# Row sums of attention weights over pairs of key chunks, added on GpSimd, in a two-layer graph-attention kernel

## Chip, cores, metric

One NeuronCore of a Trainium2 chip. The metric is the device time of one execution in microseconds (us). All runs quoted of one kernel agree within 0.3%. PE is the matmul engine (TensorE), DVE VectorE, ACT ScalarE, POOL GpSimd.

## The reference, cut to what matters

32 graphs of 512 nodes and 256 features go through two layers. Both have 8-head attention masked by the graph's adjacency; the first also has an MLP. All data is fp32, except the integer adjacency.

```python
# layer 0: allowed = (adj > 0) | (adj^T > 0) | eye ; layer 1: allowed = adj != 0
scores = einsum('bhqd,bhkd->bhqk', q * scale, k)
attn   = softmax(where(allowed, scores, -inf))
ctx    = einsum('bhqk,bhkd->bhqd', attn, v)
x = layernorm(x + ctx @ Wo.T + bo) ; x = layernorm(x + mlp(x))      # layer 0
x = layernorm(x + layer(x))                                        # after each layer
```

## The kernel before

A slot is the attention of one graph in one layer. It has eight chunks: two groups of four heads, each with four chunks of 128 keys. Scores are computed transposed (keys on partitions), so a softmax row sum is a sum over partitions, and PE makes it with a block of ones.

```python
def scores(self, layer, k):
    ...                                        # four matmuls into one PSUM tile of 4 banks
    p = work.tile([P, HPC, N], F32, tag="p", bufs=4)
    nc.scalar.activation(p, s, AF.Exp, scale=SCALE)
def masked(self, layer, k):                    # p *= 0/1 mask, on VectorE
    nc.vector.tensor_tensor(p, p, m[:, k % NQ, None, :].to_broadcast([P, HPC, N]), ALU.mult)
def product(self, layer, k):
    for j in range(HPC): nc.tensor.matmul(a[...], self.v[...], p[:, j, :], ...)   # values (psA)
    for j in range(HPC): nc.tensor.matmul(s[...], ones, p[:, j, :], ...)          # row sums (psR)
    ...                                        # after four chunks: sT, r, rT, cT divide on VectorE
def statistics(self, y, n, i):
    ...
    nc.gpsimd.tensor_scalar(rs, mv[:, 1:2], EPS, None, ALU.add)                   # rs on GpSimd
    nc.gpsimd.tensor_tensor(rs, rs, neg_half[:, 0:1], ALU.pow)
```

Every slot is interleaved with other work, so that PE has something to do while ScalarE and VectorE work on the weights. In an **MLP slot** (F in the prediction) it is the rest of another graph's layer 0: output projection, MLP, three layer norms. In a **mask slot** (O) it is the end of another graph's layer 1, and the masks of a new graph. Four slots form the cycle: mask, MLP, MLP, mask.

norm1, norm2 and norm3 are the three layer norms of layer 0, norm4 is that of layer 1; a number in brackets is one of four blocks of 128 rows. rs is the reciprocal of a row's standard deviation, which each norm waits for. bov is a bias row added to x.

## Time and profile before

| | before |
|---|---|
| median of 3 runs | 3851.9 us (3851.83 to 3852.65) |
| busy PE / DVE / ACT / POOL | 94 / 65 / 42 / 36% |
| MLP slot / mask slot | 70.3 / 49.4 and 48.3 us (two mask slots in a row) |
| granted PE clock | 0.992 |

The granted clock is the share of the full PE clock that the trace shows as granted. In these traces it is either full or half, and half comes in stretches of 3.4 us or two or three times that (at the very end of a run, other lengths). Counted over the whole trace, from the first output projection of one slot to that of the next, all 32 MLP slots of before take 70.3 us without such a stretch. Of 30 mask slots (the first and the last left out) 15 have none and take 48.3 us, and 15 have one and take 49.1 to 49.3. So the 49.4 above is a mask slot with a low clock.

The prediction below shows the lines. A line of the page's groups gives the source line, engine, operation, tiles and shapes, then busy time and mean duration, then the idle time ahead of the group and who ended it. In a timeline the first number is the start, the second the duration in us. In a chain of waits each piece is start, duration, what ran.

### The profile page before, as it was taken

How to read it: one execution, taken by the hardware profiler on the slowest of the kernel's cores; microseconds unless marked ns; L12 is line 12 of the kernel's file. 1: busy time of each engine (PE TensorE's matmuls, PEld its weight loads, DVE VectorE, ACT ScalarE, POOL GpSimd, SP SyncE). 2: the span in 40 equal slices, each digit the busy share in tenths (PEclk: the TensorE clock that was granted, in tenths of full speed). 3: DMA queues.
4: the chain of work that ended last, by engine and by line, in shares of the span. 5: the costliest groups of instructions: out<-in, count | busy, mean ns of one | idle time of the engine just before them, and what ended most of it. 6: DMA issues, size and time to landing. Idle time of an engine off the chain costs nothing.

```text
span 3851.9 us, 51652 instructions
## 1 busy us (share of the span) xinstructions
PE 3608.8 (94%) x21514; PEld 1885.4 (49%) x21514; DVE 2502.6 (65%) x3461; ACT 1603.0 (42%) x1729; POOL 1376.5 (36%) x1545
## 2 busy tenths in 40 slices
PE   6999999999999999999999999998999999999998
PEld 3544536455364554635546355453554535545354
DVE  3666675766757667576665756667576675666766
ACT  3434444434444344343443444434444344343443
POOL 1333333433334243342433424333242333424332
PEclk9999999999999999999999999999999999999999
DMA  2000000000000000000000000000000100000000
GB/s 86 17 23 13 27 12 17 23 23 17 12 17 23 22 23 6 17 28 17 23 6 17 28 17 23 6 22 23 17 23 6 33 12 17 23 6 34 12 1 12
DMA packets 57553, 75.61 MB, mean 20 GB/s; under 512 B 4448, under 2 KB 40416, under 8 KB 57312
## 3 DMA queue, kind: packets, MB, share of 16 engines
q1 hardware_dynamic: 51776, 67.90, 5.2%
q10 hardware_dynamic: 5536, 4.33, 0.4%
q8 instruction: 170, 2.79, 0.3%
q14 instruction: 71, 0.58, 0.0%
HBM read 55.45 MB, written 16.78 MB: 19 GB/s over the span
## 4 chain that ended last, share of the span: by engine, by line
PE 69%; DVE 23%; POOL 5%; ACT 2%; issue 1%; DMA 0%; ACTq 0%; DVEq 0%; POOLq 0%
PE psQK L260 12%; PE psF L391 12%; PE psH L373 12%; DVE p L282 9%; PE psS L273 8%; PE psA L295 7%; PE psV L245 6%; PE psR L303 6%; PE psO L352 5%; POOL rs L330 4%; DVE st L328 3%; DVE x L411 2%; DVE m L214 2%; ACT p L277 2%; DVE y L341 2%; PE psT L233 1%
## 5 line engine op out<-in xcount | busy, mean ns | idle before, releaser
L277 ACT ACTIVATE p<-psS 128x2048 f32<-128x2048 f32 x512 | 961.9, 1879 | 1167.1 <-PE psS L273 1167.1
L282 DVE TENSOR_TENSOR p<-p,m 128x2048 f32<-128x2048 f32 x512 | 1197.4, 2344 | 273.4 <-ACT p L277 273.4
L330 POOL TENSOR_SCALAR rs<-mv 128x1 f32<-128x1 f32 x512 | 499.2, 975 | 1115.0 <-DVE mv L329 1100.3
L295 PE MATMUL psA<-p,v 128*32 128x512 f32 x4096 | 555.8, 615 | 53.6 <-DVE p L282 53.6
L273 PE MATMUL psS<-qT,kT 32*128 32x512 f32 x4096 | 583.9, 640 | 7.1 <-ACT p L277 2.0
L303 PE MATMUL psR<-p,ones 128*32 128x512 f32 x4096 | 544.6, 604 | 0.0
L314 DVE STREAM_TRANSPOSE sT<-psR 128x512 f32<-128x512 f32 x128 | 91.3, 713 | 643.8 <-PE psR L303 643.8
L391 PE MATMUL psF<-w_L_gnn_W,hT 128*128 128x256 f32 x2048 | 459.1, 382 | 0.0
L373 PE MATMUL psH<-xT,w_L_gnn_W 128*128 128x256 f32 x2048 | 459.1, 382 | 0.0
L391 PEld LDWEIGHTS psF<-w_L_gnn_W,hT 128*128 128x128 f32 x2048 | 383.8, 190 | 100.7 <-ACT cT L311 26.8
L373 PEld LDWEIGHTS psH<-xT,w_L_gnn_W 128*128 128x128 f32 x2048 | 383.8, 190 | 98.2 <-ACT xT L236 24.3
L317 POOL TENSOR_TENSOR total<-total,sT 128x16 f32<-128x16 f32 x128 | 29.0, 227 | 985.6 <-DVE sT L314 985.6
L331 POOL TENSOR_TENSOR rs<-rs,neg_half 128x1 f32<-128x1 f32 x512 | 327.1, 639 | 42.7
L273 PEld LDWEIGHTS psS<-qT,kT 32*128 32x128 f32 x4096 | 159.9, 182 | 332.4 <-issue 187.0
L303 PEld LDWEIGHTS psR<-p,ones 128*32 128x32 f32 x4096 | 135.3, 112 | 314.7 <-issue 305.4
L381 ACT ACTIVATE hT<-psH,c_L_gnn_b 128x256 f32<-128x256 f32 x512 | 215.1, 471 | 171.3 <-PE psH L373 169.2
L260 PE MATMUL psQK<-xT,w_L_gnn_Wqkv 128*128 128x512 f32 x512 | 245.0, 611 | 0.0
L252 ACT COPY v<-psV 128x512 f32<-128x512 f32 x128 | 75.0, 586 | 403.3 <-PE psV L245 403.3
L352 PE MATMUL psO<-w_L_gnn_Wo,cT 128*128 128x256 f32 x1024 | 238.4, 386 | 0.5 <-DVE held L768 0.5
L352 PEld LDWEIGHTS psO<-w_L_gnn_Wo,cT 128*128 128x128 f32 x1024 | 189.2, 190 | 72.3 <-ACT kT L263 47.8
L341 DVE TENSOR_TENSOR y<-psO,x 128x256 f32<-128x256 f32 x256 | 104.1, 407 | 152.5 <-PE psO L352 152.5
L295 PEld LDWEIGHTS psA<-p,v 128*32 128x32 f32 x4096 | 80.9, 108 | 230.1 <-issue 101.9
(64 smaller groups left out, 3476.9 us busy)
## 6 DMA issues: line engine op xcount, KB each, us to landing
adj<-in_adj_dram SPq DMA_DIRECT2D x32, 1024.0 KB, 6.2
x<-in_x_dram SPq DMA_DIRECT2D x32, 512.0 KB, 3.9
out_dram<-x SPq DMA_DIRECT2D x32, 512.0 KB, 2.9
w_L_gnn_W<-in_L_gnn_W_dram ACTq DMA_DIRECT2D x2, 1024.0 KB, 10.8
w_L_gnn_Wqkv<-in_L_gnn_Wqkv_dram SPq DMA_DIRECT2D x1, 768.0 KB, 5.0
w_L_gnn_Wo<-in_L_gnn_Wo_dram ACTq DMA_DIRECT2D x2, 256.0 KB, 5.5
s_L_gnn_bo<-in_L_gnn_bo_dram ACTq DMA_DIRECT2D x2, 128.0 KB, 5.7
s_L_gnn_ln_g<-in_L_gnn_ln_g_dram ACTq DMA_DIRECT2D x2, 128.0 KB, 8.4
```

Source lines behind the costliest of these rows:

```text
L245: nc.tensor.matmul(ps[:, j, :], self.xT[:, i, at], proj[layer][0][2][:, i, :], start=(i == 0), stop=(i == ND - 1),)
L260: nc.tensor.matmul(ps, w[:, i, c * P : (c + 1) * P], self.xT[:, i, :], start=(i == 0), stop=(i == ND - 1))
L273: nc.tensor.matmul(s[:, j, :], self.kT[at, hg, kc * P : (kc + 1) * P], self.qT[at, hg, :], start=True, stop=True)
L277: nc.scalar.activation(p, s, AF.Exp, scale=SCALE)
L282: nc.vector.tensor_tensor(p, p, m[:, k % NQ, None, :].to_broadcast([P, HPC, N]), ALU.mult)
L295: nc.tensor.matmul(a[j * HD : (j + 1) * HD, :], self.v[:, kc, h * HD : (h + 1) * HD], p[:, j, :], start=(kc == 0), stop=(kc == NQ - 1),)
L303: nc.tensor.matmul(s[j * HD : (j + 1) * HD, :], ones, p[:, j, :], start=(kc == 0), stop=(kc == NQ - 1))
L330: nc.gpsimd.tensor_scalar(rs, mv[:, 1:2], EPS, None, ALU.add)
L331: nc.gpsimd.tensor_tensor(rs, rs, neg_half[:, 0:1], ALU.pow)
L352: nc.tensor.matmul(ps[:, j, :], self.cT[:, k, at], wo[layer][:, k, :], start=(k == 0), stop=(k == ND - 1))
L373: nc.tensor.matmul(ps[:, j, :], w1[:, c, at], self.xT[:, c, h * 2 * P : (h + 1) * 2 * P], start=(c == 0), stop=(c == ND - 1),)
L391: nc.tensor.matmul(ps, self.hT[h][:, f, j * P : (j + 1) * P], w2[:, f, :], start=(f == 0), stop=(f == NF - 1))
```

## The change

The intent: PE is busy 94% of the time, and row sums are 15% of its busy time (544.6 of 3608.8 us). GpSimd adds the weights of two chunks in place, so that one row sum serves both, for three of four pairs. Six weight buffers keep the weights long enough. To relieve VectorE, ScalarE empties the layer 1 mask from PSUM. The preparation of the mask codes goes to the end of the slot.

```diff
-                code = self.tile("edge", [NQ, N], BF16, bufs=1)
+                edge = self.tile("edge", [NQ, N], BF16, bufs=1)
+                none = self.tile("none", [NQ, N], BF16, bufs=1)
                 for i in range(NQ):
...
+                    nc.gpsimd.tensor_scalar(none[:, i, :], self.adj[:, i, :], 0.0, None, ALU.is_equal)
...
-                nc.vector.tensor_scalar(self.m1[:, i, :], ps, 0.0, None, ALU.not_equal)
+                nc.scalar.activation(self.m1[:, i, :], ps, AF.Copy, bias=1.0, scale=-1.0)
...                                  # p bufs 4 -> 6; xT, sT, rT bufs 2 -> 1; z bufs 3 -> 2
+            def pair(self, k):
+                nc.gpsimd.tensor_tensor(self.p[k], self.p[k], self.p[k + 1], ALU.add)
+            def sums(self, k, first=False, last=False):
...                                  # the ones matmuls and the division, out of product()
             # MLP slot, second half
             last.norm2(2)
             last.norm3(1)
-            g.product(layer, 4)
+            g.sums(2, last=True)     # and with it the division for heads 0 to 3
+            g.product(4)
             g.scores(layer, 7)
             last.norm2(3)
...
-            g.product(layer, 5)
             last.transpose(last.x2, 0)
-            g.product(layer, 6)
+            g.product(5)
+            g.pair(4)
             last.value(1, 0)
+            g.product(6)
             last.transpose(last.x2, 1)
-            g.product(layer, 7)
+            g.sums(6, first=True)
...
+            g.product(7)
+            g.sums(7)
+            g.sums(4, last=True)
             last.value(1, 1)
+            if later is not None:
+                later.code()         # was after residual1 (MLP slot), before the last multiply (mask slot)
...                                  # MLP slot, first half: pair(0) after product 1, pair(2) before hidden(1, ...)
...                                  # mask slot: pair(0), pair(2), pair(4) after products 0, 2, 5
```

## The prediction

> **What bounds the kernel now.** I read the page first (busy times, then the chain that ended last), then the stage table of four consecutive attention slots, the timeline of those slots, and the chain of waits inside them.
>
> ```profile
> PE 3608.8 (94%) x21514; PEld 1885.4 (49%) x21514; DVE 2502.6 (65%) x3461; ACT 1603.0 (42%) x1729; POOL 1376.5 (36%) x1545
> ...
> PE 69%; DVE 23%; POOL 5%; ACT 2%; issue 1%; DMA 0%; ACTq 0%; DVEq 0%; POOLq 0%
> ...
> L282 DVE TENSOR_TENSOR p<-p,m 128x2048 f32<-128x2048 f32 x512 | 1197.4, 2344 | 273.4 <-ACT p L277 273.4
> L330 POOL TENSOR_SCALAR rs<-mv 128x1 f32<-128x1 f32 x512 | 499.2, 975 | 1115.0 <-DVE mv L329 1100.3
> ...
> L303 PE MATMUL psR<-p,ones 128*32 128x512 f32 x4096 | 544.6, 604 | 0.0
> ```
>
> PE looks like the bound (94% busy), but 28% of the chain is DVE and POOL. A one-element POOL instruction (L330) averages 975 ns, so POOL is waiting inside its own instructions. The program has 64 slots (32 graphs, two layers), in a cycle of four: two that carry another graph's MLP (F) and two that carry a new graph's masks (O). The stage table has, per slot: span, then busy PE, PEld, DVE, ACT, POOL, and the granted clock; its last line is 8 us inside an O slot.
>
> ```profile
> 1999.86:2070.24 70.38, 68.63 (x389) 40.51 (x385) 42.74 (x68) 28.97 (x36) 24.46 (x30) 1.00 0.07 23
> 2140.49:2189.89 49.40, 44.88 (x293) 18.58 (x289) 35.77 (x40) 21.07 (x18) 20.70 (x18) 0.97 0.04 11
> 2189.89:2238.20 48.31, 43.23 (x290) 18.13 (x289) 35.39 (x40) 21.07 (x18) 14.78 (x14) 1.00 0.04 12
> ...
> 2166.00:2174.00 8.00, 6.05 (x39) 2.54 (x32) 8.00 (x7) 1.88 (x1) 4.48 (x4) 0.79 0.01 3
> ```
>
> An F slot is PE bound except for some 7 us of DVE chain after the MLP. In an O slot the chain runs on DVE and POOL without a break from 2191.83 to 2221.14, 29.3 of 48.3 us: PE waits there. So PE time saved in O is worth nothing, and DVE time is worth everything. Now the timeline of the same O slot (start, duration):
>
> ```profile
> 2202.19 2.37 POOL L169 TENSOR_TENSOR x<-x,bov 128x1024 f32<-128x1024 f32 x1
> 2204.64 4.48 POOL L169 TENSOR_TENSOR x<-x,s_L_gnn_ln_b 128x1024 f32<-128x1024 f32 x1
> ...
> 2202.26 2.46 DVE L411 TENSOR_SCALAR x<-y,mv,rs 128x256 f32<-128x256 f32 x1 [0.45 <-POOL rs L331]
> 2204.63 2.28 DVE L282 TENSOR_TENSOR p<-p,m 128x2048 f32<-128x2048 f32 x1
> 2206.83 0.68 DVE L214 TENSOR_SCALAR m<-psM 128x512 bf16<-128x512 f32 x1
> ...
> 2208.03 3.24 DVE L282 TENSOR_TENSOR p<-p,m 128x2048 f32<-128x2048 f32 x1
> ```
>
> L411 normally takes 0.41 us; begun just after the POOL add, it ends with it, after 2.46. The second POOL add needs 4.48 instead of 2.37 because the DVE multiply (2.28) began first; the next multiply takes 3.24 instead of 2.28 because it waits for that add. L214, which reads PSUM, is not held up. The two engines take turns, whole instruction by whole instruction.
>
> **What the Trainium skill says.** "SBUF — State Buffer", section "Who interferes with whom": a DVE instruction with two SBUF inputs, or in a two-port mode, and a GpSimd instruction that reads SBUF exclude each other; the later one blocks until the first is done. The lines above agree. "GPSIMD Engine Reference", section 3.1: a 2048-element fp32 add takes 4497 ns on GpSimd. The trace has 2.36 us for 1024 elements and 0.22 us for 16, so about 2.12 ns per element and 4.5 us for 2048, an estimate that agrees. "TensorE: Matmul & The Clock Gate", Part 1: an idle PE loses half its clock, and needs activity to get it back. The 0.79 above, after 2 us of idle PE, agrees in kind: there a product and its row sum took 3.3 us instead of 1.86.
>
> **The change part by part.**
> 1. Row sums: eight chunks per slot become five products. In the chain one is 0.86 us, so 3 x 0.86 = 2.6 us of PE per slot, 165 us in all, if nothing else binds.
> 2. Adds: three per slot, 4.5 us each: 13.5 us per slot, 864 us over the run. Each shuts out the mask multiplies, the affine steps (L336, L337), the two-port normalizations (L404, L411) and cT (L321).
> 3. Layer 1 mask: 4 x 0.60 us leave DVE in an O slot (2.4 us on the chain), 0.59 us each arrive on ScalarE (42% busy): free.
> 4. "none": four POOL passes of 1.03 us more per graph. The whole code, 8.2 us, moves to the end of a slot, so it stands in the POOL queue ahead of the next O slot's first rs.
> 5. The division for the first four heads (sT, r, rT, cT: 2.4 us of DVE) moves in F from the idle stretch at 2030 to behind the second paired sum, so into the busy DVE stretch after the MLP.
> 6. Six p buffers: no wait for a p buffer shows before, so no gain by themselves.
>
> *F slot, walked by hand* on the times of the slot at 1999.86. The first row sum saved brings nothing: the third score product waits for exp (1.89 us at 2004.71) anyway; the second brings 0.45. The first add follows rs of tile 3 at 2013.1 and holds the port to 2017.75, so the last affine ends at 2018.7 and the transpose starts 0.3 later than before. The third saved sum makes mlp(3) end 0.5 us earlier, at 2045.5. Then DVE: first x2 tiles to 2048.6, the moved division to 2051.0, norm2(3) and the multiply for chunk 6 end at 2054.9 (2052.92 before). rs of tile 3 ends at 2055.6 and the third add follows at once, to 2060.1; norm3(3) waits for it exactly as L411 does above, so the second x2 transpose starts at 2060.5. Left on PE: 0.45 transpose, 3 x 0.86 sums, 3.63 query/key, 1.0 product, 1.73 value, with gaps 9.5: end 2070.0 against 2064.47. **+5.5 us.**
>
> *O slot*, from its first score product S (2134.71 in the first one). Before, the last m1 ends at S+37.6. Now the code passes and the multiply for chunk 0 alternate to S+10.7, the multiply for chunk 1 ends at S+13.0, then the add of bov (layer 1 slots only) at S+15.4, so norm4(1) ends at S+17.95 (before S+13.3). Chunk 2 ends at S+22.2. The first add takes S+22.95 to 27.45, with norm4(3) behind it. Then turns: chunk 3 to 29.9, residual add to 32.3, chunk 4 to 34.5, residual add to 36.9, chunk 5 to 39.1, second add to 43.6. Only then the paired sum on PE (44.5), which the DVE division waits for. The third add starts when r is in (S+45.8) and lasts to 50.4; cT, chunk 6 and m0 of tile 3 end at S+54.0, and the value product needs that PSUM buffer. PE tail: 1.73 + 1.0 + 0.86 + 3.63 + 1.0 + 2 x 0.86 + 1.73 = 11.7, end S+65.8 against S+49.4. **+16.4 us**; in the other O slot, without bov, about +14.8.
>
> Sum: 32 x 5.5 = 176; 31 x 15.6 = 484; lower PE clock after 4.5 to 6.5 us of idle PE, some 1.4 us (3.3 - 1.86) in each O and half that often in F: 65. Total 725 us: 4577, rounded to **4560 us**.
>
> **The rivals.** *A, PE stays the bound and the adds hide on a POOL that is 36% busy:* 3852 - 165 and up to 80 more for the shorter DVE chain: 3610 to 3690. For it: 94% PE, and much of POOL's 1376 us is waiting. Against it: the port, not POOL, is what is scarce, and the waiting POOL time is the proof. *B, the adds collide only in part*, because they settle into the DVE-free half of the F slot (2018 to 2034 has few two-input DVE instructions) and only the O slots lose, some 8 us each: near 4100. For it: the second F add does fall there. Against: the third F add starts right behind the rs that norm3(3) also waits for, and there is no free stretch in O. *C, port plus clock:* long PE idles keep the clock low through most O slots: up to 4800.
>
> **Range and chances.** The walk has errors of perhaps 2 us per F slot and 4 per O slot, mostly shared by all slots: 4380 to 4720. Slower by over 2%: 0.93; within 2%: 0.03; faster: 0.04 (rival A, if the exclusion were weaker for these adds than for L169).
>
> **What would show it.** L303 with 2560 matmuls instead of 4096. A new POOL add, 128x2048, with an uncontended time of 4.5 us and a mean above 6. L282's mean up from 2344 to over 3000 ns, L404 and L411 well over 1000. PE busy share down to about 80%, DVE and POOL shares of the chain far up, F slots near 76 us and O slots near 64. The prediction is wrong if L282 keeps 2.3 us beside a running add, if the adds fall where DVE has no two-input work, or if an add takes much less than 4.5 us.

## The result

The changed kernel takes 4573.7 us (median of 4 runs, 4572.74 to 4574.72) against 3851.9 us in the same rounds. The ratio is 1.187 (95% interval 1.185 to 1.189): it is 19% slower.

From the page of the changed kernel: busy times, chain shares, and the groups that answer to those of before (multiply, the new add, row sums):

```profile
PE 3706.6 (81%) x19978; PEld 1901.0 (42%) x19978; DVE 3160.4 (69%) x3333; ACT 1667.7 (36%) x1857; POOL 2592.1 (57%) x1865
...
DVE 41%; PE 41%; POOL 14%; issue 2%; DVEq 0%; POOLq 0%
...
L284 DVE TENSOR_TENSOR p<-p,m 128x2048 f32<-128x2048 f32 x512 | 1492.8, 2921 | 134.0 <-ACT p L279 134.0
...
L306 POOL TENSOR_TENSOR p<-p,p 128x2048 f32<-128x2048 f32 x192 | 1001.1, 5214 | 6.9 <-PE psA L292 4.3
...
L314 PE MATMUL psR<-p,ones 128*32 128x512 f32 x2560 | 381.0, 690 | 22.4 <-POOL p L306 22.4
```

The row sums fell from 4096 matmuls to 2560 as intended, but PE is only busy 81%, and it is busy longer in all. The multiply grew by 577 ns on average. DVE's share of the chain went from 23 to 41%, POOL's from 5 to 14%.

The stage table, slot by slot (span, busy PE, PEld, DVE, ACT, POOL, granted clock, DMA): mask, MLP, MLP, and the mask slot that came before these three.

```profile
2305.08:2367.10 62.02, 44.98 (x269) 19.14 (x268) 45.45 (x37) 23.18 (x22) 39.64 (x25) 0.86 0.03 9
2367.10:2445.51 78.41, 70.34 (x364) 40.19 (x364) 51.89 (x69) 28.89 (x36) 39.42 (x33) 0.93 0.06 21
2445.51:2523.91 78.40, 70.25 (x362) 40.17 (x361) 53.25 (x68) 28.88 (x36) 41.06 (x34) 0.93 0.02 7
...
2240.60:2305.08 64.48, 45.68 (x265) 19.17 (x264) 47.43 (x36) 23.17 (x22) 42.04 (x27) 0.87 0.08 25
```

Both kinds of slot got longer: the MLP slot from 70.3 to 78.4 us, the mask slots from 48.3 and 49.4 to 62.0 and 64.5. The clock fell too: from 1.00 to 0.93 in MLP slots, from 1.00 and 0.97 to 0.86 and 0.87 in mask slots, and from 0.992 to 0.904 over the run. Every slot of the changed kernel has a low stretch.

Where the time sits is seen in the timeline of one mask slot (POOL lines, then DVE lines):

```profile
2261.45 4.51 POOL L306 TENSOR_TENSOR p<-p,p 128x2048 f32<-128x2048 f32 x1
...
2272.63 6.58 POOL L306 TENSOR_TENSOR p<-p,p 128x2048 f32<-128x2048 f32 x1
...
2283.18 4.50 POOL L306 TENSOR_TENSOR p<-p,p 128x2048 f32<-128x2048 f32 x1
...
2261.51 4.60 DVE L418 TENSOR_SCALAR x<-y,mv,rs 128x256 f32<-128x256 f32 x1 [0.45 <-POOL rs L338]
...
2275.34 6.01 DVE L284 TENSOR_TENSOR p<-p,m 128x2048 f32<-128x2048 f32 x1
...
2283.71 4.53 DVE L328 TENSOR_TENSOR cT<-cT,rT 128x512 f32<-128x512 f32 x1
```

Each of the three adds has a DVE instruction that starts after it and ends just when the add (or, for the multiply, the add and the multiply itself) is done. L418 needs 0.41 us by itself, L328 0.69. The second add waited 2.07 us for the multiply before it, which is not shown (6.58 instead of 4.51), and the next multiply waited 3.8 us for that add.

And in the chain of waits of an MLP slot, from the third add on:

```profile
2428.53 4.59 DVE x L411
...
2433.17 0.90 PE psT L235 x3
2434.07 1.87 PE psR L314 x8
2435.94 4.94 PE psQK L262 x8
```

The third add ran from 2428.47 to 2432.97; the last normalization (L411) waited for it, and PE for the normalization. After this pause the row sum takes 1.87 us (0.86 before the change) and the query and key products 4.94 (3.63 before the change). The granted clock from 2428.5 to 2441.0 is 0.60.

### The profile page after: what moved, and what is told of

It is laid out like the page before. It is cut to its first block, busy times and chain, and to the rows that moved or that the text cites. A ratio compares the mean times of both kernels' runs of the same rounds, so it can differ in the third digit from the quotient of the medians.

```text
span 4572.0 us, 48806 instructions
## 1 busy us (share of the span) xinstructions
PE 3706.6 (81%) x19978; PEld 1901.0 (42%) x19978; DVE 3160.4 (69%) x3333; ACT 1667.7 (36%) x1857; POOL 2592.1 (57%) x1865
## 4 chain that ended last, share of the span: by engine, by line
DVE 41%; PE 41%; POOL 14%; issue 2%; DVEq 0%; POOLq 0%
DVE p L284 14%; PE psF L398 10%; PE psQK L262 8%; PE psR L314 5%; PE psH L380 5%; DVE cent L343 4%; POOL rs L337 4%; POOL none L197 4%; PE psV L247 4%; DVE cT L328 4%; DVE x L418 3%; PE psA L292 3%; DVE x L411 3%; PE psS L275 3%; DVE st L335 3%; POOL rs L338 2%
## 5 line engine op out<-in xcount | busy, mean ns | idle before, releaser
L284 DVE TENSOR_TENSOR p<-p,m 128x2048 f32<-128x2048 f32 x512 | 1492.8, 2921 | 134.0 <-ACT p L279 134.0
L306 POOL TENSOR_TENSOR p<-p,p 128x2048 f32<-128x2048 f32 x192 | 1001.1, 5214 | 6.9 <-PE psA L292 4.3
L337 POOL TENSOR_SCALAR rs<-mv 128x1 f32<-128x1 f32 x512 | 471.9, 922 | 833.3 <-DVE mv L336 819.2
L292 PE MATMUL psA<-p,v 128*32 128x512 f32 x4096 | 592.1, 652 | 74.5 <-DVE p L284 74.5
L314 PE MATMUL psR<-p,ones 128*32 128x512 f32 x2560 | 381.0, 690 | 22.4 <-POOL p L306 22.4
L247 PE MATMUL psV<-w_L_gnn_Wqkv,xT 128*128 128x256 f32 x512 | 179.0, 511 | 222.2 <-DVE m L216 222.2
L235 PE MATMUL psT<-ident,x 128*128 128x128 f32 x768 | 167.0, 329 | 212.9 <-DVE x L411 111.9
L348 DVE TENSOR_TENSOR y<-psF,x 128x256 f32<-128x256 f32 x128 | 54.4, 425 | 360.7 <-PE psF L398 360.7
L343 DVE SCALAR_TENSOR_TENSOR cent<-y,mv,s_L_gnn_ln_g 128x256 f32<-128x256 f32 x256 | 256.6, 1002 | 0.0
L235 PEld LDWEIGHTS psT<-ident,x 128*128 128x128 f32 x768 | 96.0, 158 | 378.3 <-DVE y L348 127.2
```

The source lines that it names most:

```text
L292: nc.tensor.matmul(self.acc[hg][j * HD : (j + 1) * HD, :], self.v[:, kc, h * HD : (h + 1) * HD], self.p[k][:, j, :], start=(kc == 0), stop ...
L306: nc.gpsimd.tensor_tensor(self.p[k], self.p[k], self.p[k + 1], ALU.add)
L314: nc.tensor.matmul(self.total[j * HD : (j + 1) * HD, :], ones, self.p[k][:, j, :], start=first, stop=last)
L343: nc.vector.scalar_tensor_tensor(c, y, stats[0], g, ALU.subtract, ALU.mult)
```

## The experiments

The theory: the adds and the DVE instructions that the prediction names (those with two inputs in SBUF, and the normalizations, which it calls two-port) exclude each other, the places of the adds are on DVE's chain, and PE time is hardly worth anything there. The rivals: PE time is what counts; GpSimd is just slow, so whoever waits for its results or stands behind them in its line waits long; or the new order, not the adds, costs.

| run | median us | ratio to before |
|---|---|---|
| before | 3850.9 to 3852.1 | 1 |
| changed | 4573.7 | 1.187 |
| a_no_adds | 3988.2 | 1.036 |
| b_fills | 4267.0 | 1.108 |
| c_no_third | 4296.7 | 1.116 |
| d_code_back | 4523.7 | 1.175 |
| e_adds_dve | 4133.5 | 1.073 |
| f_mask_scalar | 3799.5 | 0.987 |
| g_division_early | 4518.3 | 1.173 |
| h_one_pair | 3773.0 | 0.980 |
| i_dummy_free | 3851.5 | 1.000 |
| j_dummy_tail | 3955.5 | 1.027 |
| k_fewer_sums | 3836.3 | 0.996 |
| l_buffers | 3852.2 | 1.000 |

### What the saving is worth: k_fewer_sums

```diff
-                for j in range(HPC):              # row sums, in the kernel before
+                for j in range(HPC) if k not in (1, 2, 5) else ():
```

> The kernel before with the row sums of chunks 1, 2 and 5 simply left out (five instead of eight per slot, as in the change; wrong result on purpose), nothing added. It prices the saving by itself. Theory (saved PE time counts only where PE sets the end): in an MLP slot 0.45 us for chunk 1 (exp ends soon after), 0.86 for chunk 2, nothing for chunk 5 and nothing in a mask slot: 32 x 1.3 = 42 us less, 3810, 3790 to 3830; more PE idle may cost some of it through the clock. Rival (PE busy 94% is the bound): 165 us less, 3687.

Measured: 3836.3 us, 15.7 us less (ratio 0.9961, 0.9947 to 0.9975). The rival's 165 us are excluded, and even the theory's 42 were too many. Two consecutive MLP slots with the two mask slots between them, from the stage table:

```profile
2057.92:2127.00 69.08, 66.06 (x364) 39.67 (x361) 42.74 (x68) 28.74 (x36) 26.79 (x34) 1.00 0.07 24
...
2223.59:2294.30 70.71, 67.69 (x365) 39.86 (x361) 42.73 (x68) 28.73 (x36) 24.44 (x30) 0.98 0.07 23
```

The first MLP slot saved 1.2 of the 1.3 us that the walk gave; the other was not shorter than before, at a clock of 0.98. The two mask slots took 48.3 us each, as one without a low clock does before. Over the trace, 9 of the 32 MLP slots are like the first (69.1 us) and 23, with a low stretch, like the other (70.6 to 70.7): together they save only 2 us. All 30 mask slots take 48.3 us, though 23 of them have a low stretch; that none takes 49.3 us any more saves 15. So PE time is worth nothing in a mask slot at full clock, and what little was won came from the mask slots with a low clock, where the theory did not look. In the order of the kernel before, these row sums at no cost for the adds are worth 0.4%. That is no limit for other orders: in h_one_pair below, without low stretches, one row sum per MLP slot brings more than all three do here.

### The adds taken away: a_no_adds

```diff
-                nc.gpsimd.tensor_tensor(self.p[k], self.p[k], self.p[k + 1], ALU.add)
+                pass                              # wrong sums, on purpose
```

> The changed kernel without its three GpSimd adds per slot (the paired row sums then cover only one chunk, so the result is wrong on purpose); schedule, saved row sums, ScalarE mask and buffers stay. Theory (the adds shut out the vector engine): the whole loss goes away, but the moved division (2.4 us on the chain of an MLP slot) and the code passes at the start of a mask slot use up what the row sums save: 3830 us, 3780 to 3880. Rival 1 (the saved row sums are worth their PE time once the adds are gone): 3610 to 3700. Rival 2 (it is the new order, not the adds, that loses): over 4300.

Measured: 3988.2 us. So 585 of the 722 us are the adds (with the low clock that comes with them), and rival 2 falls as the main cause. But the rest did not go down to 3830: all but the adds, with fewer row sums, is still 3.6% slower than before. Its slots in the stage table, one MLP slot and one mask slot:

```profile
2070.91:2143.53 72.62, 68.45 (x364) 39.86 (x361) 42.62 (x68) 28.85 (x36) 24.31 (x30) 0.98 0.07 22
...
2216.07:2268.51 52.44, 44.37 (x269) 18.42 (x265) 35.87 (x36) 23.13 (x22) 26.73 (x24) 0.90 0.09 31
```

PE pauses 2.0 us for the multiply of chunk 6, which the moved division delays. Then a row sum takes 1.86 us instead of 0.86 and the query and key products 4.34 instead of 3.63: 1.7 us, on top of what the expectation reckoned with. In the mask slot the value product after its pause takes 3.2 us instead of 1.7 to 2.0. The low clock, 0.961 over the run against 0.992, was left out of the expectation. The pauses of PE in that MLP slot, in its timeline:

```profile
2121.22 1.99 PE L247 MATMUL psV<-w_L_gnn_Wv,xT 128*128 128x256 f32 x8 [0.73 <-ACT xT L238]
2125.24 1.06 PE L292 MATMUL psA<-p,v 128*32 128x512 f32 x8 [2.03 <-DVE p L284]
...
2126.91 1.94 PE L314 MATMUL psR<-p,ones 128*32 128x512 f32 x8
```

The slot shown is not every slot: 18 of the 32 MLP slots have the same pauses and no low stretch, and take 71.0 us; the other 14 take 72.5 to 72.6. The clock is only part of the 136 us. The mask slot shown is 4.1 us longer than one without a low stretch before: norm4(1) ends 2.7 us later, behind the code passes, one row sum more (0.9) stands at the end, the low clock costs some 1.9 on the value product and the product after it (3.18 + 1.44 instead of 1.73 + 1.00), and the ScalarE mask gives 1.2 back. By these figures the low clock comes to some 65 us, about half of the 136: 14 x 1.5 in MLP slots and 31 x 1.9 in mask slots, less the 15 x 1.0 of before, an estimate.

### Same GpSimd time, nothing read: b_fills

```diff
-                nc.gpsimd.tensor_tensor(self.p[k], self.p[k], self.p[k + 1], ALU.add)
+                for j in (slice(0, 4), slice(0, 4), slice(0, 2)):   # wrong on purpose
+                    nc.gpsimd.memset(self.p[k][:, j, :], 1.0)
```

> As the changed kernel, but each add is replaced by three GpSimd fills of the same tile (2048 + 2048 + 1024 elements, about 4.5 us together from 0.83 ns per element): the same GpSimd time, the same dependencies of the row sums, but nothing read. Wrong result on purpose. Theory (exclusion of reads): the multiplies keep 2.3 us instead of 2.9, the single-input normalizations of the x2 rows are still shut out if the write port counts for them: 4150 to 4250 us; if they are not shut out, near the kernel without adds. Rival (GpSimd is simply a slow engine in line, port or not): 4570 as the changed kernel.

Measured: 4267.0 us, between the kernel without adds and the changed kernel. The groups of the multiply, the fills and the affine step, and from the timeline a place's fills with a multiply that starts beside them:

```profile
L284 DVE TENSOR_TENSOR p<-p,m 128x2048 f32<-128x2048 f32 x512 | 1242.6, 2432 | 129.4 <-ACT p L279 129.4
...
L307 POOL MEMSET p<- 128x2048 f32 (+1 forms) x576 | 877.0, 1523 | 26.0 <-PE psA L292 3.9
...
L344 DVE SCALAR_TENSOR_TENSOR cent<-y,mv,s_L_gnn_ln_g 128x256 f32<-128x256 f32 x256 | 119.9, 468 | 0.0
...
2113.38 4.70 POOL L307 MEMSET p<- 128x2048 f32 x3
...
2115.25 2.27 DVE L284 TENSOR_TENSOR p<-p,m 128x2048 f32<-128x2048 f32 x1
```

The fills take 877.0 / 192 = 4.57 us per place, as an add does. The multiply has 2432 ns here, as without any adds (2436), and 2921 with adds; the affine step has 468, with adds 1002. The multiply shown runs beside two of the fills and is not held up at all, so the shorter pieces are not the reason. So it is the reading of GpSimd that shuts out these instructions: that part of the theory is shown. Yet the fills still cost 279 us over the kernel without adds, which the theory put down to the normalizations. It is only partly so. The first fill (1.81 us) does hold up the last normalization: 1.86 us instead of 0.41. Of the 279 us, 165 are in the mask slots (58.5 and 56.3 us, against 52.5 and 51.3 without adds), and there a long wait of DVE shows in this line of a timeline:

```profile
2133.55 0.72 DVE L322 STREAM_TRANSPOSE sT<-psR 128x512 f32<-128x512 f32 x1 [8.26 <-PE psR L315]
```

DVE stands idle for 8.26 us, because the division waits for a row sum, and this for a fill that stands in GpSimd's line behind another fill and two residual adds (PE's waits for the fills add up to 216 us over the run). So the rival of the line is right for part of the cost. The two causes hide each other: in the changed kernel DVE is shut out in the same stretch in which it waits here. They can't be added up to the 585 us.

### The third add undone: c_no_third

```diff
-            g.pair(4)
-            g.sums(4, last=True)
+            g.sums(4)
+            g.sums(5, last=True)
```

> The changed kernel without its third pair (chunks 4 and 5 get row sums of their own; right result). By the walk the third add stands on the chain in both slots: 4.5 us before norm3(3) in an MLP slot and 4 us before cT in a mask slot, and most of the low clock follows the first. Expected 4260 us, 4200 to 4340, though PE has 55 us more row sums. Rival (PE waits for the results of the adds): the third add's result is waited for nowhere, so it would be some 50 us slower: 4620.

Measured: 4296.7 us, 277 less than changed, with more row sums. Nobody waits for the result of this add, so the rival of the waited-for result falls for it; what it costs, it costs by whom it shuts out. The two groups in question fall back to 935 and 400 ns (with the third add 1891 and 1442, in the kernel before 1112 and 400):

```profile
L328 DVE TENSOR_TENSOR cT<-cT,rT 128x512 f32<-128x512 f32 x128 | 119.7, 935 | 13.3
...
L411 DVE TENSOR_SCALAR x<-z,mv,rs 128x256 f32<-128x256 f32 x128 | 51.2, 400 | 14.6 <-POOL rs L338 14.3 <-issue 0.3
```

### The adds on VectorE: e_adds_dve

```diff
-                nc.gpsimd.tensor_tensor(self.p[k], self.p[k], self.p[k + 1], ALU.add)
+                nc.vector.tensor_tensor(self.p[k], self.p[k], self.p[k + 1], ALU.add)
```

> The changed kernel with the adds on VectorE instead of GpSimd (right result). Each takes 2.3 us instead of 4.5 and cannot shut itself out. By the walk only two adds of a mask slot lie on the chain, 31 x 4.4 = 136 us over the kernel without adds: 3970 us, 3900 to 4040. Rival (any engine's adds cost the same because VectorE is the bound): 4570 or more.

Measured: 4133.5 us. It is 145 us above the kernel without adds; the expectation had 136 for this step, and missed the total by the same error as in a_no_adds. That the step agrees is partly luck: the mask slots got 4.0 and 3.1 us longer, not 4.4, and the MLP slots lost 28 us, as now all 32 of them have a low stretch. Still, 512 us of adds on VectorE, the bottleneck of the mask slots, cost a quarter of what the same adds cost on GpSimd (585 us).

### One useless add, at two places: i_dummy_free, j_dummy_tail

```diff
+    spare = const.tile([P, HPC * N], F32, name="spare")           # kernel before, MLP slot
             last.residual1()
             if later is not None: later.code()
+            nc.gpsimd.tensor_tensor(spare, spare, spare, ALU.add)  # i_dummy_free
...
             last.norm2(3)
+            nc.gpsimd.tensor_tensor(spare, spare, spare, ALU.add)  # j_dummy_tail
```

> The kernel before with one useless GpSimd add of 128 x 2048 per MLP slot on a spare tile, right after residual1, where VectorE has no two-input work until the division 9 us later. Theory (only what is shut out on the chain costs): 3852 to 3860 us, the same. Rival (an add costs by its GpSimd time, 32 x 4.5 = 144 us): 3996.

> The same useless add, 32 of them, put behind the rs of the last z tile in the MLP slot, where the third add of the change stands. Theory: norm3(3) waits 4 us, then the multiply for chunk 7, which the last product waits for; PE loses 3.5 us per slot and perhaps 1 to 2.7 us more by the low clock: 3964 to 4050. Rival (a GpSimd add that nobody's result depends on is hidden): 3852.

Measured: 3851.5 us for the first, the same as before (0.9999, 0.998 to 1.002), and 3955.5 for the second, 103.6 us more. The instruction is the same, 32 times each, and no result depends on it. In the timeline of the second:

```profile
2101.44 3.59 POOL L492 TENSOR_TENSOR spare<-spare 128x2048 f32<-128x2048 f32 x1
...
2101.50 3.68 DVE L406 TENSOR_SCALAR x<-z,mv,rs 128x256 f32<-128x256 f32 x1 [0.45 <-POOL rs L333]
```

The normalization takes 3.68 instead of 0.41 us. The MLP slot takes 2.4 us more where the clock stays full (12 slots, 72.8 us) and 4.1 more where a low stretch follows (20 slots, 74.4): part of the delay is hidden, and the clock adds to the rest. The total came out just below the expected range; this add, with one tile for both inputs, takes 3.59 us and not 4.5, and 0.9 us in 32 slots would account for it. This pair of runs shows most plainly that the place of the add decides: its time is 3.6 us at both.

### Parts of the order: d_code_back, g_division_early

```diff
             last.residual1()                       # d_code_back
+            if later is not None: later.code()
...                                                 # mask slot: code after pair(4), before masked 7
             g.product(3)                           # g_division_early
+            g.sums(2, last=True)
             last.mlp(0)
...
-            g.sums(2, last=True)
             g.product(4)
```

> The changed kernel with the eight GpSimd mask-code passes put back where they stood before (after residual1 in the MLP slot, before the last multiply in the mask slot), behind the adds. By the traces a mask slot's norm4(1) ends 2.7 us later than before where bov comes first and about 2 us otherwise, because the passes stand ahead of its rs: 31 x 2.3 = 70 us less, 4500, 4470 to 4540. Rival (the passes are hidden wherever they stand): 4573.

> The changed kernel with the second paired row sum, and so the division for the first four heads, moved ahead of the first mlp product in the MLP slot. VectorE's stretch after the MLP gets 2.4 us shorter, PE reaches its end 0.86 us later: 32 x 1.5 = 50 us less, 4525, 4490 to 4560. Rival (the division is hidden in the wait for the third add): 4573 to 4600.

Measured: 4523.7 us for the first, 50 less than changed, and 4518.3 for the second, 55 less. Both are within their ranges, but not slot by slot as expected. With the code passes put back, the mask slots that have the add of bov get 2.8 us shorter and the others 0.6. With the division early, the MLP slots get 1.8 and 2.6 us shorter, and of the two mask slots after them one 0.4 us shorter and the other 1.4 longer. Together they are small against the adds.

### Parts alone, and what is left: l_buffers, f_mask_scalar, h_one_pair

```diff
-                p = work.tile([P, HPC, N], F32, tag="p", ..., bufs=4)     # l_buffers, kernel before
+                p = work.tile([P, HPC, N], F32, tag="p", ..., bufs=6)     # also xT, sT, rT 1, z 2
...
-                nc.vector.tensor_scalar(self.m1[:, i, :], ps, 0.0, None, ALU.not_equal)   # f_mask_scalar
+                nc.scalar.activation(self.m1[:, i, :], ps, AF.Copy, bias=1.0, scale=-1.0) # with "none"
...                                                                         # h_one_pair = f, and in MLP slots:
             last.residual1()
+            g.product(layer, 2, True)              # no row sum of its own
+            nc.gpsimd.tensor_tensor(g.p[2], g.p[2], g.p[3], ALU.add)
             if later is not None: later.code()
-            g.product(layer, 2)
...
-            g.product(layer, 3)
+            g.product(layer, 3, True)              # row sum of the pair
             last.mlp(0)
```

> The kernel before with the change's buffers alone: six for the weights, one each for xT, sT and rT, two for z. Theory: no wait for a weight buffer stands in the trace of before, 3852, 3845 to 3860. Rival (the cut of the other buffers is what costs): over 3900.

> The kernel before with one part of the change alone: layer 1 masks emptied by ScalarE, with the extra GpSimd passes where the code stood. 4 x 0.60 us leave the VectorE chain of each of 31 mask slots: 74 us less, 3778, 3765 to 3810. Rival (PE is the bound at 94%, VectorE time is worth nothing): 3852.

> The kernel before with the ScalarE mask, and with a single GpSimd add per MLP slot, chunks 2 and 3, put into the stretch where VectorE has nothing with two inputs; the division stays where it was. Theory (only the place of an add matters): 32 x 0.86 = 28 us less than with the ScalarE mask alone, 3750, 3735 to 3785. Rival (each add costs VectorE time wherever it stands): over 3800.

Measured: 3852.2 us for the buffers alone, no difference. The ScalarE mask alone gives 3799.5 us, 51 less than before (ratio 0.987, 0.985 to 0.988), so it is the one part of the change that pays by itself, but less than the 74 expected. All its mask slots take 47.1 us, 1.2 less than one without a low stretch before. The chain of such a slot shows why. Only three of the four layer 1 evacuations were on the chain (the value product waits for the last layer 0 one), and 0.6 of these 1.8 us are given back here:

```profile
2123.72 2.20 DVE p L284
2125.92 0.60 DVE m L216
2126.52 3.77 DVE p L284
```

The second multiply took 3.16 us in the chain of before. It now asks for the port 0.6 us sooner, while the residual add of GpSimd ends when it did. The 1.2 us make 36 of the 51; the other 15 are the low stretches of before, 15 x 1.0 us, of which no slot of this run has any (clock 0.999).

With one add per MLP slot at the free place, h_one_pair takes 3773.0 us: 26.5 us less than the ScalarE mask alone, where 32 x 0.86 = 27.5 were to be had. It takes 2.0% less than the kernel before (ratio 0.978 to 0.981: clear of the noise), is correct, and is the fastest of all. Its MLP slots all take 69.5 us at full clock. Its add is undisturbed and disturbs nobody: the affine step (468 ns), cT (1113) and both normalizations (400 and 889) have the times of before.

```profile
L473 POOL TENSOR_TENSOR p<-p,p 128x2048 f32<-128x2048 f32 x32 | 145.2, 4537 | 0.0
```

## Why the prediction was right, point by point

The time was predicted to within 14 us (4560 against 4573.7), in the middle of the range. That closeness is partly luck. The walk's own sum is 4577, which the prediction calls 4560 after rounding. And two errors nearly cancelled: over the whole trace the MLP slots lost 258 us, where the walk and its clock term had 198, the mask slots 447, where they had 527, and the start-up, which the walk left out, 14.

- **The exclusion and its places: shown.** The add's least time is 4489 ns (estimated 4.5). Every one of its predicted collisions is in the trace: the first add ahead of the last affine step in the MLP slot, the third ahead of norm3(3); in the mask slot the adds stand ahead of norm4(3), of a multiply, and of cT. b_fills shows that it is the reading that shuts out the multiplies; i and j show that the place decides.
- **"PE time saved in O is worth nothing": shown** by k_fewer_sums for mask slots at full clock (48.3 us with and without the row sums). In those with a low stretch it saved 1.0 us, which the walk did not have. The walk's 1.3 us per MLP slot came in 9 of 32 slots; in the other 23 the low clock took it all.
- **MLP slot: +8.2 us instead of 5.5 plus half of 1.4.** The walk of the waits is right to 0.2 us at this point: norm3(3) was to end, and the transpose to start, 60.6 us after the first projection product (2060.5 - 1999.9), and it starts 60.4 after it. The term that was mis-sized is the lower clock. It was put at 1.4 us in every second slot; it is there in all 32 MLP slots, and in the chain shown it comes to 0.4 (transpose) + 1.0 (row sum) + 1.3 (query and key) = 2.7 us.
- **Mask slot: +15.1 and +13.7 us instead of 16.4 and 14.8, each plus 1.4.** The port was reckoned too dear. norm4(1) ended at S+16.0 (S is the slot's first score product, as in the prediction) instead of S+17.95, because the code passes end at S+9.4 and the add of bov comes ahead of the multiply, not behind it. After the first add, a residual add and not the multiply went first, so the turns came in another order, and the second add was done before chunk 5's multiply and not after it. m0 of tile 3 ended at S+50.4 instead of S+54.0. The lower clock again cost more than 1.4: the value product alone took 3.78 us instead of 1.73. And the 49.4 us of before that the walk starts from hold a low stretch of 1.0 us already.
- **Code passes: right sum, wrong terms.** Eight passes of 1.03 us were assumed. The edge pass takes 0.61 us undisturbed (1.03 was a mean with waits), the "none" pass 1.48; four of each are 8.4 us.
- **ScalarE mask: the step "2.4 us on the chain" failed**; f_mask_scalar saved 1.2 us on the chain of a mask slot (three evacuations of 0.6 us, of which 0.6 us went back to a wait for the port), and the clock gave the rest of its 51 us.
- **Division and buffers:** the 2.4 us are in the trace, and g and l agree with their steps in the total.
- **What the profile was to show:** 2560 matmuls, PE 81%, L404 and L411 (now L411 and L418) at 1442 and 1426 ns, all as said. The multiply's mean of 2921 ns stays just below the "over 3000", and the add's 5214 below the "above 6", because more of the adds found the port free: 127 of 192 took 4.5 to 4.6 us.
- **The rivals.** A is excluded by k. B was right about the second add of the MLP slot, and h_one_pair makes use of just that. C did not come about in full, but its clock term is larger than the walk's 65 us: with 2.7 us in 32 MLP slots and about 2 in 31 mask slots some 150 us, an estimate.

Open: how the 585 us of the adds split between shutting out and standing in GpSimd's line, as the two overlap in time. Only the third add was taken out by itself; the first two were not priced apart. Of the 136 us that remain without adds, the code passes and the division were measured only inside the changed kernel (50 and 55 us); that about half is the clock is an estimate from the slots of one trace. What the clock costs was not tested apart in any run.

## What to carry to other kernels

Before moving work to an idle-looking engine, ask which port it shares, and look in the timeline for instructions that take far longer than their least time: a one-element instruction with a mean of 975 ns was the warning here. Price the saving by itself first (leave the work out and accept a wrong result): 165 us of a 94% busy engine were worth 16 here, and in part because the engine's clock fell where it had less to do. If the work must be moved, put it where the other engine has nothing that needs the port: the same add cost nothing at one place and 2.4 to 4.1 us at another.

## What the Trainium skill lacked or had wrong

- "SBUF — State Buffer", "Who interferes with whom": the exclusion is as described (multiply 2432 ns beside fills, 2921 beside adds). What it lacks is what happens when several instructions of one engine follow each other: here the port went to the waiting engine at the end of each. Behind three fills in a row a normalization waited only for the first (1.86 us), behind one long add for all of it (4.60 us). In this case three short instructions held up the other engine less than one long one.
- "GPSIMD Engine Reference", section 3.1: the 4497 ns for a 2048-element fp32 add agree (least 4489). Not on the page: with the same tile as both inputs the add takes 3.59 us; and a compare of 512 int32 elements to bf16 takes 1.48 us where a min and a max in one instruction take 0.61.
- "TensorE: Matmul & The Clock Gate", its closing table, asks for no idle gaps above about 3 us. Here gaps of 0.7 and 2.0 us within some 5 us (a_no_adds) were followed by a row sum at half speed (1.86 us instead of 0.86) in 14 of 32 MLP slots, and by none in the other 18. So shorter gaps can lower the clock too, but need not; a single gap of 1.6 us, in each of the 32 MLP slots of the kernel before, never did.
